# Two fused transformer layers on one core: layer-1 queries and position scores in an early pool, keys on Pool, experts three steps later

## The chip, the cores and the metric

The kernel runs on one core of a Trainium2 chip. The time is device microseconds (us) of that core for one execution of the whole program, with all inputs in the chip's own memory at the start and the output written back to it at the end. Engines are named as the profile names them: PE (TensorE, with PEld for its weight loads), DVE (VectorE), ACT (ScalarE), POOL (GpSimd) and SP (SyncE, which here only issues transfers, in the order of its own queue).

## What is computed

The input is two batches of 1024 tokens with 128 features, float32 throughout. Two layers follow each other, and each adds attention and a mixture of experts, both taken from the same normalized input, to that input.

```python
xn = _layernorm(x, axis=-1)
x = x + _L0_attn_ref(xn, ...) + _L0_ffn_ref(xn, ...)
xn = _layernorm(x, axis=-1)
x = x + _L1_attn_ref(xn, ...) + _L1_ffn_ref(xn, ...)
```

Layer 0's attention has 16 heads of 8 features, sigmoid scores and a causal mask; its experts are 32, computed densely and weighted, and one shared expert. Layer 1's attention is a softmax over all 1024 keys with a position term that depends on the clipped distance of query and key:

```python
att_rel_pos = jnp.einsum('bhsd,pd->bhsp', q, pos_emb_k)
att_idxs = jnp.clip(ar[None, :] - ar[:, None], -r, r - 1) % P     # r = 128, P = 256
att_pos = att_rel_pos[:, :, ar[:, None], att_idxs]
att = jax.nn.softmax((attn_val + att_pos) * attn_scale, axis=-1)
```

Layer 1's experts are 16 with 4 chosen for each token, and a shared expert of 352 hidden features that every token passes through.

## The kernel before, in words

**Order of the work.** Every PE instruction is placed by hand (`manual_schedule` for PE). The other engines are scheduled by a planner from the dependences, so their queues can stand in another order than the text; each engine then executes its own queue strictly in order. The program has two PE loops.

**The first loop** counts steps c. Each of the first 192 (`N_ATT`) makes one tile of layer 0's attention (`scores0`, `values0`) and opens or closes units of a feed-forward block. A unit (`open_unit`, L333) is a pair of products of 512 tokens with up to 128 hidden features (L341, L342), a sigmoid on ACT and two products on DVE; `close_unit` (L358) multiplies the result with the second weight and accumulates (L367). Units without biases (L346 to L349) are those of layer 1's shared expert, twelve in all: three parts for each of four blocks of 512 tokens. A dictionary `extra` (filled by `at(c, f, ...)`) says which other functions run at which step, and `due` says how many units may be open by then.

After step 192 comes the transition: `added0` and `merged0` of batch 1 add layer 0's two outputs and normalize again (L235 writes the normalized `xn1`), the pool `l0` is closed and `l1` opened on the same memory (`opened1`, which also clears sixteen `negmax` tiles on POOL, L776), and layer 1's attention is prepared. That preparation is what a dictionary `begin` lists for negative steps; the last loop lines before `manual_schedule` spread it over the steps up to `LAST`.

**Layer 1's attention** runs in the second loop, 128 steps (16 groups of one batch, one of four head sets and one half of the queries; 8 key tiles each). Four heads are computed at once, in four row groups of PE. A step t does:

- `scores` of its key tile: transposes of `near` (L936) and products of queries and keys (L946), then exponentials on ACT (L953);
- `values` of the step before (L965);
- `scan` of a tile ten steps ahead (`LEAD` = 10): products of queries and keys (L885), whose row maxima DVE takes, with `near` added where query and key are close (L905), or straight from PSUM (L910). `augment` (L920, L924) puts the maxima into the queries as an extra feature.

**Where `near` comes from.** `positions(n, pair)` multiplies queries with position vectors (L845), copies the result to `rel` on ACT (L849), fills its tail on DVE (L851), writes it to a scratch tensor in memory (`bounce`, L858) and reads it back skewed (`near`, L864). The last two are transfers on SP's queue, and the second waits for the landing of the first. Step 8n - 13 + 4 pair has the positions of group n, except that those of (1, 1) are at step 0.

**Operands.** `projections(b)` makes queries, keys and values of a batch; `operands(b, s)` makes one head set's masked queries `qs` (L820), two keys `kls` and `khs` (L824) on DVE and values `vs` on POOL (L827). In the second loop it stands 17 steps ahead of its group.

**Layer 1's experts.** Routing (`gate1`, `sort1`) is a sequence of small DVE operations, let go piece by piece. Then POOL scatters every token to its four slots (L618, two each step from `SCATTER` on), and at step `EXPERTS` the attention pauses: PE computes 79 blocks of 128 slots, each with weights that POOL fetches with an indirect transfer (L660). Tokens are loaded four blocks at a time on SP's queue (`fetch_x`, L670) and results stored there (L714). From then on POOL gathers the results, 64 in all (L630), scales and adds them (L640, L641). `paced` ties each scatter and gather to the last exponential of its step. When a quarter of the tokens (half of batch 0) is complete, `result` (L646) stores it, again on SP's queue.

Of the kernel before, what the change touches and what calls it, by code (L numbers as in the profile page):

```python
# [10 lines left out]
F32 = mybir.dt.float32  # L11
# [6 lines left out]
P = 128  # L18
D = 128
# [27 lines left out]
def fused_layers_kernel(ctx: ExitStack, tc: tile.TileContext, a: dict, out: bass.AP):  # L47
# [41 lines left out]


    banks = psum_pools(3, 1, 1, 0)
    l0_pool = tc.tile_pool(name="l0", bufs=1)
    l0 = l0_pool.__enter__()

# [238 lines left out]
    def open_unit():  # L333

        (m, wa, wb, w2m, ba, bb, rows), xT, tok = units[len(opened)][:3]
        if rows is not None:
            cb = moe.tile([P, TB], F32, tag="cb", name="cb", bufs=3)
            for lo, hi, src in rows:
                nc.sync.dma_start(cb[lo:hi, :], src[tok:tok + TB].partition_broadcast(hi - lo))
        hh = big()  # L340
        nc.tensor.matmul(hh[0:m, 0, :], wa, xT, start=True, stop=True)  # L341
        nc.tensor.matmul(hh[0:m, 1, :], wb, xT, start=True, stop=True)  # L342
        sg = moe.tile([P, TB], F32, tag="sg", name="sg")
        t = moe.tile([P, TB], F32, tag="t", name="t")
        h = moe.tile([P, TB], F32, tag="h", name="h", bufs=4)
        if ba is None:  # L346
            nc.scalar.activation(sg[0:m], hh[0:m, 0, :], AF.Sigmoid)
            nc.vector.tensor_mul(t[0:m], hh[0:m, 0, :], sg[0:m])
            nc.vector.tensor_mul(h[0:m], hh[0:m, 1, :], t[0:m])  # L349
        else:  # L350
            nc.scalar.activation(sg[0:m], hh[0:m, 0, :], AF.Sigmoid, bias=ba)  # L351
            nc.vector.scalar_tensor_tensor(t[0:m], hh[0:m, 0, :], ba, sg[0:m], ALU.add, ALU.mult)  # L352
            nc.vector.scalar_tensor_tensor(h[0:m], hh[0:m, 1, :], bb, t[0:m], ALU.add, ALU.mult)  # L353
        if rows is not None:
            nc.gpsimd.tensor_mul(h[0:m], h[0:m], cb[0:m])  # L355
        opened.append(h)
# [436 lines left out]
        return slice(32 * r, 32 * r + 32)  # L793

    def projections(b):
        l1 = pools["l1"]
        qf = l1.tile([P, T], F32, tag="qf", name="qf")
        kf = l1.tile([P, T], F32, tag="kf", name="kf")
        v = l1.tile([P, NT, D], F32, tag="vf", name="vf")
        for q in range(NB):  # L800
            c = slice(q * TB, (q + 1) * TB)
            ps = small()
            nc.tensor.matmul(ps, wq, xT1[b][:, c], start=True, stop=True)
            nc.scalar.mul(qf[:, c], ps, 1.0 / math.sqrt(HD))
            ps = small()
            nc.tensor.matmul(ps, wk, xT1[b][:, c], start=True, stop=True)
            nc.vector.tensor_copy(kf[:, c], ps)
            ps = quads(small())
            for i in range(4):
                t = q * TB + i * P  # L810
                nc.tensor.matmul(ps[:, i, :], xT1[b][:, t:t + P], wv, start=True, stop=True)
            nc.scalar.copy(v[:, 4 * q:4 * q + 4, :], ps)
        full[b] = qf, kf, v

    def operands(b, s):

        l1 = pools["l1"]
        qf, kf, v = full[b]
        qs = l1.tile([P, T], F32, tag="qs", name="qs", bufs=2)
        nc.vector.tensor_scalar(qs, qf, mask[:, s:s + 1], None, ALU.mult)  # L820
        ks = []
        for i, name in enumerate(("kls", "khs")):
            t = l1.tile([P, T], F32, tag=name, name=name, bufs=2)
            nc.vector.tensor_scalar(t, kf, not_aux[:, s:s + 1], k_add[:, i, s:s + 1], ALU.mult, ALU.add)  # L824
            ks.append(t)
        vs = l1.tile([P, NT, D], F32, tag="vs", name="vs", bufs=2)
        nc.gpsimd.tensor_copy(vs, v)  # L827
        ones = vs.rearrange("p t (r c) -> p t r c", r=NG)[:, :, :, aux[s]:aux[s] + 1]
        nc.gpsimd.memset(ones, 1.0)
        head[b, s] = qs, ks[0], ks[1], vs  # L830

    n_rel = [0]

    def positions(n, pair):


        b, s, q = groups[n]
        l1 = pools["l1"]
        qs = head[b, s][0]
        ps = [t.rearrange("p (j w) -> p j w", j=2) for t in four_banks()]  # L840
        for j in range(2):
            t = q * TB + (2 * pair + j) * P
            for r in range(NG):
                g = rows_of(r)
                nc.tensor.matmul(ps[r][:, j, :], qs[g, t:t + P], posd[g, :], start=True, stop=True)  # L845
        rel = l1.tile([P, 2 * NG * NEAR], F32, tag="rel", name="rel")
        rel = rel.rearrange("p (j r w) -> p j r w", j=2, r=NG)
        for r in range(NG):
            nc.scalar.copy(rel[:, :, r, 0:2 * RAD], ps[r])  # L849
        for j in range(2):  # L850
            nc.vector.tensor_copy(  # L851
                rel[:, j, :, 2 * RAD:NEAR],
                rel[:, j, :, 2 * RAD - 1:2 * RAD].to_broadcast([P, NG, NEAR - 2 * RAD]),
            )
        for j in range(2):
            bounce = bounces[n_rel[0] % N_BOUNCE]
            n_rel[0] += 1
            nc.sync.dma_start(  # L858
                bounce[:, :, P - 1:P - 1 + NEAR].rearrange("r p w -> p r w"), rel[:, j, :, :]
            )  # L860
            slot = (4 * n + 2 * pair + j) % 10
            t = pools["l1" if slot < 6 else "late"].tile([P, NG, NEAR], F32, tag=f"near{slot}", name="near")
            skew = bass.AP(bounce.tensor, bounce.offset + P - 1, [[W - 1, P], [P * W, NG], [1, NEAR]])
            nc.sync.dma_start(t, skew)  # L864
            near[n, 2 * pair + j] = t

    def spans(lo, hi, cut):

# [140 lines left out]
    for n, (b, s, q) in enumerate(groups):  # L1009
        t0 = 8 * n - LEAD  # L1010
        if q == 0:
            if s == 0:
                at_step(t0 - 8, projections, b)
            at_step(t0 - 7, operands, b, s)
        for pair in range(2):

            at_step(0 if (n, pair) == (1, 1) else 8 * n - 13 + 4 * pair, positions, n, pair)
    for n, (b, s, q) in enumerate(groups):
        for m in range(8):
            if 8 * n - LEAD + m < 0:  # L1020
                at_step(8 * n - LEAD + m, scan, n, m // 2, m % 2)
    at_step(-2, augment, 0)


    gates = {}
# [46 lines left out]
        at(60 + 4 * i, regroup, i)  # L1072

    at(N_ATT, blocks1, 0)
    at(N_ATT + 2, added0, 1)
    at(N_ATT + 4, merged0, 1)
    at(N_ATT + 5, lambda: l0_pool.__exit__(None, None, None))
    at(N_ATT + 5, opened1)
    at(N_ATT + 9, turned1, 1)
    at(N_ATT + 9, blocks1, 1)  # L1080
    LAST = N_ATT + 22
    for t in sorted(begin):
        if t < 0:
            for f, args in begin[t]:
                at(LAST + t * (LAST - N_ATT - 6) // -min(begin), f, *args)

    with tc.manual_schedule(engines={mybir.EngineType.PE}):
        c = 0
        while c < LAST or closed[0] < len(units):
            for f, args in extra.get(c, ()):  # L1090
                f(*args)
            if c < N_ATT:
                scores0(c)
                due = max(0, c - U0 + 1)
                if due > HALF:
                    due = HALF + (due - HALF) * HALF // (N_ATT - U0 - HALF)
            else:
                due = len(units)
            fresh = len(opened) < due
            if fresh:  # L1100
                open_unit()
            if 0 < c <= N_ATT:
                values0(c - 1)
            if closed[0] < len(opened) - 2 or (not fresh and c >= N_ATT and closed[0] < len(opened)):
                close_unit()
            for entry in list(later):
                entry[0] -= 1
                if entry[0] < 0:
                    later.remove(entry)
                    entry[1](*entry[2])  # L1110
            c += 1
        for _, f, args in later:
            f(*args)
# [16 lines left out]

    SORT, SCATTER, EXPERTS = 1, 26, 8 * len(groups) // B
    aside = {}

    def beside(t, f, *args):
# [11 lines left out]
                return  # L1148

    for t in range(SORT, SCATTER - 1):  # L1150
        for i in range(1 + t % 2):
            beside(t, route_on)
    beside(SCATTER - 1, route_on, True)
    for i in range(NTT * K1):
# [4 lines left out]
        beside(EXPERTS - 1, fetch_w, i)  # L1159

    with tc.manual_schedule(engines={mybir.EngineType.PE}):
        for t in range(N_STEPS + 1):
            if t == EXPERTS:
                values(t // 8 - 1, NT - 1, whole)
                experts()
            before = begin.get(t, ())
            for f, args in before:
# [4 lines left out]


            n, kt = (t - 1) // 8, (t - 1) % 8
            halved = 0 < kt and t + 1 < N_STEPS and not is_near(t + 1) and not before
            if t and t != EXPERTS:
                values(n, kt, left if halved else whole)
            m = t + LEAD
# [79 lines left out]
```

## Time and profile before

Five runs: median 1355.3 us, from 1347.06 to 1363.21.

| what | value |
|---|---|
| time of the profiled execution | 1355.62 us |
| its span, first to last instruction | 1353.8 us |
| mean granted PE clock | 0.960 |
| PE busy | 1221.7 us (90%) |
| DVE busy | 781.9 us (58%) |
| ACT busy | 617.1 us (46%) |
| POOL busy | 417.5 us (31%) |
| last layer-0 attention matmul starts | 436.1 us |
| step 0 of layer 1's attention starts | 523.4 us |
| first expert matmul (transposes, L685) | 883.6 us |
| step 64, right after the experts | 1031.0 us |

Times in the table's last four rows are from the start of the span. Busy time counts compute instructions only; matmuls are pipelined and their ends are modelled, so a busy PE is not PE at its peak. In the timelines, a bracket at the end of a line gives how long the engine stood idle before it and what released it; `x8` means eight instructions merged into one line. SPq lines are issues on SP's queue, and their length is not that of the transfer. The granted clock is a share of full speed.

### The profile page before, as it was taken

The numbers are of one execution on the slowest core, as the hardware profiler recorded it, in microseconds if no ns is written. First come the engines' busy times: TensorE is split into PE (matmuls) and PEld (weight loads), VectorE is DVE, ScalarE is ACT, GpSimd is POOL, SyncE is SP. The second block draws the span as 40 slices with busy tenths as digits, with TensorE's granted clock in tenths as the row PEclk, the third lists the DMA queues.
The fourth block names the chain that finished last, engine by engine and source line by source line (L and its number), as shares of the span: only waits on it lengthen the run. The fifth ranks groups of instructions, "written<-read, shape, count | busy, mean of one in ns | idle before, by whom it ended". The sixth has DMA issues, their size and how long they took to land.

```text
span 1353.8 us, 22925 instructions
## 1 busy us (share of the span) xinstructions
PE 1221.7 (90%) x8567; PEld 578.9 (43%) x8567; DVE 781.9 (58%) x2211; ACT 617.1 (46%) x1086; POOL 417.5 (31%) x514
## 2 busy tenths in 40 slices
PE   5889999989999888898999999968899999979997
PEld 2323332333333435344444344468886444434443
DVE  7773333563333775868765656734455866656553
ACT  3634444535454322453554545433344554536453
POOL 1124243233332100000033433135553445545540
PEclk9889999999999996898998999989999999989998
DMA  6773121111110064453455554578883555455430
GB/s 176 187 208 83 57 59 52 39 32 47 41 49 21 1 206 124 138 177 113 143 167 172 187 191 139 185 234 253 256 260 99 176 164 178 135 185 167 153 104 17
DMA packets 142499, 181.76 MB, mean 134 GB/s; under 512 B 16436, under 2 KB 126260, under 8 KB 142132
## 3 DMA queue, kind: packets, MB, share of 16 engines
q1 hardware_dynamic: 131972, 147.30, 35.8%
q0 software_dynamic: 10416, 32.99, 7.8%
q8 instruction: 68, 1.11, 0.3%
q14 instruction: 43, 0.35, 0.1%
HBM read 110.81 MB, written 73.77 MB: 136 GB/s over the span
## 4 chain that ended last, share of the span: by engine, by line
PE 37%; DMA 8%; DVE 8%; issue 5%; ACT 3%; POOL 2%; SPq 0%; POOLq 0%; DVEq 0%; ACTq 0%
PE sm L946 10%; PE sm L885 8%; PE acc L965 8%; PE sm L936 6%; DVE maxima L910 3%; DMA bounce<-rel 3%; DMA near<-bounce 3%; PE sm L845 2%; DVE junk L905 2%; POOL blockw L660 2%; PE sm L695 1%; ACT p L953 1%; DMA blockw<-wx,weight_row 1%; POOL room L660 1%; ACT rel L849 1%
## 5 line engine op out<-in xcount | busy, mean ns | idle before, releaser
L953 ACT ACTIVATE p<-sm 128x512 f32<-128x512 f32 x512 | 265.0, 607 | 254.1 <-PE sm L946 245.5
L910 DVE TENSOR_REDUCE maxima<-sm 128x1 f32<-128x512 f32 (+3 forms) x472 | 226.6, 502 | 100.5 <-PE sm L885 97.4
L455 ACT ACTIVATE at<-big 128x1024 f32<-128x1024 f32 (+1 forms) x192 | 144.8, 808 | 150.8 <-PE big L449 145.0
L905 DVE CUSTOM_DVE_ANT_0 junk<-sm,near 128x384 f32<-128x384 f32 (+2 forms) x292 | 130.4, 446 | 64.8 <-PE sm L885 42.4
L965 PE MATMUL acc<-p,vs 128*32 128x512 f32 (+1 forms) x1288 | 146.8, 525 | 0.4 <-ACT yu L977 0.4
L355 POOL TENSOR_TENSOR h<-h,cb 128x512 f32<-128x512 f32 x64 | 83.3, 1301 | 196.6 <-DVE h L353 186.4
L936 PE MATMUL sm<-ident,near 128*128 128x128 f32 x704 | 110.1, 291 | 32.4 <-DVE maxima L905 17.8
L352 DVE SCALAR_TENSOR_TENSOR t<-big,b,sg 128x512 f32<-128x512 f32 x64 | 47.9, 749 | 158.2 <-ACT sg L351 158.2
L946 PE MATMUL sm<-qa,kls 32*128 32x512 f32 (+3 forms) x832 | 121.2, 565 | 0.0
L660 POOL DMA_INDIRECT blockw<-wx,weight_row x53 | 50.4, 952 | 215.9 <-DVE rel L851 165.1
L936 PEld LDWEIGHTS sm<-ident,near 128*128 128x128 f32 x704 | 79.6, 146 | 81.6 <-issue 36.5
L885 PE MATMUL sm<-kls,qs 32*128 32x512 f32 (+2 forms) x776 | 111.0, 576 | 2.6 <-DVE at L560 1.5
L618 POOL DMA_INDIRECT slots_x<-xn,slot_of x64 | 62.9, 983 | 143.2 <-ACT p L953 133.1
L449 PE MATMUL big<-qm,xT 32*128 32x512 f32 (+3 forms) x768 | 103.5, 554 | 3.2 <-ACT at L455 1.9
L475 PE MATMUL acc<-at,xn 128*32 128x512 f32 (+3 forms) x768 | 84.9, 515 | 5.6 <-POOL at L460 4.5
L341 PE MATMUL big<-xT,w 128*128 128x512 f32 x128 | 73.9, 660 | 16.0 <-DVE h L353 13.6
L849 ACT COPY rel<-sm 128x512 f32<-128x512 f32 x116 | 59.6, 600 | 62.4 <-PE sm L845 56.7
L640 POOL TENSOR_SCALAR got<-got,share 128x128 f32<-128x128 f32 x64 | 41.5, 649 | 123.0 <-DMA got<-slots_y,slot_of 122.6
L630 POOL DMA_INDIRECT got<-slots_y,slot_of x64 | 64.7, 1011 | 30.9 <-ACT p L953 19.7
L367 PE MATMUL ffn<-h,w 128*128 128x512 f32 x128 | 72.9, 652 | 0.0
L460 POOL TENSOR_SCALAR_AFFINE_SELECT at<-at 128x512 f32<-128x512 f32 x64 | 40.8, 638 | 101.2 <-ACT at L455 100.9
L885 PEld LDWEIGHTS sm<-kls,qs 32*128 32x128 f32 x776 | 38.3, 186 | 78.3 <-ACT p L953 16.4
(285 smaller groups left out, 1709.1 us busy)
## 6 DMA issues: line engine op xcount, KB each, us to landing
bounce<-rel SPq DMA_DIRECT2D x64, 768.0 KB
near<-bounce SPq DMA_DIRECT2D x64, 768.0 KB
cb<-cw SPq DMA_DIRECT2D x128, 128.0 KB
slots_x<-zeros SPq DMA_DIRECT2D x19, 256.0 KB
room<-slots_x SPq DMA_DIRECT2D x19, 256.0 KB
slots_y<-by SPq DMA_DIRECT2D x19, 256.0 KB
bounce<-zeros SPq DMA_DIRECT2D x40, 63.5 KB
w<-in_w_dram SPq DMA_DIRECT2D x2, 1024.0 KB
```

The costliest lines, as they stand in the source:

```text
L355: nc.gpsimd.tensor_mul(h[0:m], h[0:m], cb[0:m])
L449: nc.tensor.matmul(halves[r // 2][:, r % 2, off:TB], xT0[b][g, kt * P:(kt + 1) * P], masked[b, s][g, q * TB + off:(q + 1) * TB], start=Tru ...
L455: nc.scalar.activation(at[:, 2 * j:2 * j + 2, off:TB], sc[:, :, off:TB], AF.Sigmoid, scale=4.0 / math.sqrt(HD))
L475: nc.tensor.matmul(y[32 * r:32 * r + 32, off:TB], xn0[b][:, kt * P + 32 * r:kt * P + 32 * r + 32], at[:, r, off:TB], start=(kt == 0), stop ...
L660: nc.gpsimd.indirect_dma_start(t[:, 0:WX], None, wx[:, :], bass.IndirectOffsetOnAxis(ap=weight_row[:, i:i + 1], axis=0))
L885: nc.tensor.matmul(ps[r][:, (k0 - lo) * P:(k1 - lo) * P], qs[g, qt * P:(qt + 1) * P], (kh if far else kl)[g, k0 * P:k1 * P], start=True, s ...
L905: nc.vector.tensor_tensor_reduce(junk[:, 0:(k1 - k0) * P], part, near[n, i][:, r, w0:w0 + (k1 - k0) * P], 1.0, -BIG, ALU.add, ALU.max, mx[ ...
L910: nc.vector.tensor_reduce(mx[:, r, slot:slot + 1], part, AX.X, ALU.max)
L936: nc.tensor.matmul(ps[r][:, i * P:(i + 1) * P], near[n, i][:, r, w0:w0 + P], ident, is_transpose=True, start=(i == close[0]), stop=False, ...
L946: nc.tensor.matmul(ps[r][:, i0 * P:i1 * P], k[g, kt * P:(kt + 1) * P], qa[n][g, i0 * P:i1 * P], start=(m == 0 and not close), stop=(m == l ...
L953: e = nc.scalar.activation(p[:, r, :], ps[r], AF.Exp)
L965: nc.tensor.matmul(y[rows_of(r), part], vs[:, kt, rows_of(r)], probs[n, kt][:, r, part], start=(kt == 0), stop=(kt == NT - 1 and part.stop ...
```

## The change

It has these parts:

- A pool `early`, opened ahead of layer 0's, holds `qf`, `kf`, the projected values, `qs` and `rel`, which were in `l1`. So `projections(0)`, `queries(0, 0)` and the first three `by_position` stand ahead of `opened1` now.
- `operands` is split into `queries` and `operands`, and `positions` into `by_position` (up to the write of the bounce) and `near_by` (reading it back). Positions of (1, 1) are made in the transition; only their `near_by` is left ahead of step 0.
- The preparation has steps of its own instead of being spread; scans, one each step, alternate with units (`due`).
- A unit without biases copies its second factor on ACT and makes its last product on POOL, instead of two products on DVE.
- The keys of all head sets are made on POOL instead of DVE, and `kf` is copied on ACT.
- Routing is let go more slowly, `SCATTER` is 33 instead of 26 and `EXPERTS` 67 instead of 64; gathers and results, counted from `EXPERTS`, move with it.

```diff
+    early = ctx.enter_context(tc.tile_pool(name="early", bufs=1))
...
             nc.scalar.activation(sg[0:m], hh[0:m, 0, :], AF.Sigmoid)
-            nc.vector.tensor_mul(t[0:m], hh[0:m, 0, :], sg[0:m])
-            nc.vector.tensor_mul(h[0:m], hh[0:m, 1, :], t[0:m])
+            nc.scalar.copy(t[0:m], hh[0:m, 1, :])
+            nc.vector.tensor_mul(sg[0:m], hh[0:m, 0, :], sg[0:m])
+            nc.gpsimd.tensor_mul(h[0:m], t[0:m], sg[0:m])
...
-        qf = l1.tile([P, T], F32, tag="qf", name="qf")
-        kf = l1.tile([P, T], F32, tag="kf", name="kf")
-        v = l1.tile([P, NT, D], F32, tag="vf", name="vf")
+        qf = early.tile([P, T], F32, tag="qf", name="qf")
+        kf = early.tile([P, T], F32, tag="kf", name="kf")
+        v = early.tile([P, NT, D], F32, tag="vf", name="vf")
...
-            nc.vector.tensor_copy(kf[:, c], ps)
+            nc.scalar.copy(kf[:, c], ps)
...
+    def queries(b, s):
+
+        qs = early.tile([P, T], F32, tag="qs", name="qs", bufs=2)
+        nc.vector.tensor_scalar(qs, full[b][0], mask[:, s:s + 1], None, ALU.mult)
+        head[b, s] = (qs,)
+
     def operands(b, s):
...
-        qs = l1.tile([P, T], F32, tag="qs", name="qs", bufs=2)
-        nc.vector.tensor_scalar(qs, qf, mask[:, s:s + 1], None, ALU.mult)
...
-            nc.vector.tensor_scalar(t, kf, not_aux[:, s:s + 1], k_add[:, i, s:s + 1], ALU.mult, ALU.add)
+            nc.gpsimd.tensor_scalar(t, kf, not_aux[:, s:s + 1], k_add[:, i, s:s + 1], ALU.mult, ALU.add)
...
-    def positions(n, pair):
+    def by_position(n, pair):
...
-            bounce = bounces[n_rel[0] % N_BOUNCE]
+            bounce = bounce_of[n, pair, j] = bounces[n_rel[0] % N_BOUNCE]
             n_rel[0] += 1
             nc.sync.dma_start(
                 bounce[:, :, P - 1:P - 1 + NEAR].rearrange("r p w -> p r w"), rel[:, j, :, :]
             )
+
+    def near_by(n, pair):
+
+        for j in range(2):
+            bounce = bounce_of.pop((n, pair, j))
             slot = (4 * n + 2 * pair + j) % 10
...
+    def positions(n, pair):
+        by_position(n, pair)
+        near_by(n, pair)
...
+            at_step(t0 - 7, queries, b, s)
             at_step(t0 - 7, operands, b, s)
         for pair in range(2):
-
-            at_step(0 if (n, pair) == (1, 1) else 8 * n - 13 + 4 * pair, positions, n, pair)
...
+            at_step(8 * n - 13 + 4 * pair, positions, n, pair)
...
     at(N_ATT, blocks1, 0)
+    at(N_ATT, projections, 0)
+    at(N_ATT, queries, 0, 0)
+    at(N_ATT + 1, by_position, 0, 0)
     at(N_ATT + 2, added0, 1)
+    at(N_ATT + 2, by_position, 0, 1)
     at(N_ATT + 4, merged0, 1)
     at(N_ATT + 5, lambda: l0_pool.__exit__(None, None, None))
     at(N_ATT + 5, opened1)
-    at(N_ATT + 9, turned1, 1)
+    for pair in range(2):
+        at(N_ATT + 5, near_by, 0, pair)
+    at(N_ATT + 5, operands, 0, 0)
+    at(N_ATT + 5, by_position, 1, 0)
+    at(N_ATT + 6, near_by, 1, 0)
+    at(N_ATT + 8, turned1, 1)
     at(N_ATT + 9, blocks1, 1)
-    LAST = N_ATT + 22
...
+    for m in range(LEAD):
+        at(N_ATT + 7 + m, scan, m // 8, m % 8 // 2, m % 2)
+    at(N_ATT + 9, by_position, 1, 1)
+    at(N_ATT + 12, queries, 0, 1)
+    at(N_ATT + 12, operands, 0, 1)
+    LAST = N_ATT + 7 + LEAD
+    at(LAST - 2, augment, 0)
...
-                due = len(units)
+                due = 2 * HALF + (min(max(c - N_ATT - 1, 0), 2) if c < N_ATT + 7 else c - N_ATT - 4)
+            due = min(due, len(units))
...
-    SORT, SCATTER, EXPERTS = 1, 26, 8 * len(groups) // B
+    SORT, SCATTER, EXPERTS = 1, 33, 8 * len(groups) // B + 3
...
-        for i in range(1 + t % 2):
+        for i in range(1 + (t % 4 == 0)):
             beside(t, route_on)
...
+        near_by(1, 1)
         for t in range(N_STEPS + 1):
             if t == EXPERTS:
-                values(t // 8 - 1, NT - 1, whole)
+                values((t - 1) // 8, (t - 1) % 8, whole)
                 experts()
...
-            halved = 0 < kt and t + 1 < N_STEPS and not is_near(t + 1) and not before
+            halved = 0 < kt and t != EXPERTS and t + 1 < N_STEPS and not is_near(t + 1) and not before
```

## The prediction

> **What bounds the kernel now.** I read the page first, then busy time by stretch, then the timelines of PE, DVE, SP and POOL around the two places that the change moves.
>
> ```profile
> span 1353.8 us, 22925 instructions
> PE 1221.7 (90%) x8567; PEld 578.9 (43%) x8567; DVE 781.9 (58%) x2211; ACT 617.1 (46%) x1086; POOL 417.5 (31%) x514
> ```
>
> PE is the bound over the whole, so what counts is where PE stands idle or cold. Stretches (us; PE, PEld, DVE, ACT, POOL busy; granted clock; DMA share; GB/s):
>
> ```profile
> 457.90:483.10 25.20, 22.82 (x90) 11.30 (x90) 14.56 (x22) 10.27 (x17) 5.09 (x20) 0.93 0.33 96
> 483.10:523.40 40.30, 31.76 (x150) 14.53 (x151) 33.65 (x112) 5.34 (x11) 0.00 (x0) 0.76 0.56 175
> 523.40:885.00 361.60, 334.77 (x2705) 159.57 (x2705) 248.38 (x796) 177.79 (x341) 72.97 (x77) 0.95 0.49 158
> ```
>
> The last layer-0 attention matmul runs at 436.1, step 0 of layer 1 begins at 523.4: a transition of 87.3 us. In 483.1 to 523.4 DVE is busy 33.65 of 40.3 and PE waits for it at a clock of 0.76.
>
> The timelines of DVE, SP and PE say what starts that stretch and what ends it:
>
> ```profile
> 455.65 2.14 DVE L235 TENSOR_SCALAR xn<-x,ln_mv,ln_rstd 128x128 f32<-128x128 f32 x8
> ...
> 483.09 0.42 DVE L905 CUSTOM_DVE_ANT_0 junk<-big,near 128x256 f32<-128x256 f32 x1 [3.45 <-DMA near<-bounce]
> ```
> ```profile
> 473.33 0.94 SPq L858 DMA_DIRECT2D bounce<-rel  x2
> 477.76 3.74 SPq L864 DMA_DIRECT2D near<-bounce  x2
> ```
> ```profile
> 523.42 1.94 PE L936 MATMUL sm<-ident,near 128*128 128x128 f32 x8 [2.54 <-issue]
> ```
>
> The second norm (L235) ends at 457.8; only then is the l0 pool closed, l1 opened and the projections evacuated. Rel is ready at 473.3, and the first scan's `near` lands at 483.1. Ten scans follow on DVE.
>
> At the experts, SP (in order) and PE show:
>
> ```profile
> 889.62 4.85 SPq L864 DMA_DIRECT2D near<-bounce  x2
> 894.58 0.51 SPq L670 DMA_DIRECT2D room<-slots_x  x1
> ...
> 902.79 1.11 PE L685 MATMUL sm<-ident,room 128*128 128x128 f32 x4 [9.83 <-DMA room<-slots_x]
> ```
>
> `positions` of step 63 puts two bounce and two near transfers between the second and the third `fetch_x`; PE stands 9.83 us.
>
> In batch 1 the same queue is held again, by `result` waiting for POOL (timelines of POOL, SP and PE):
>
> ```profile
> 1180.51 0.45 POOL L641 TENSOR_TENSOR x<-x,got 128x128 f32<-128x128 f32 x1
> ```
> ```profile
> 1180.99 0.38 SPq L646 DMA_DIRECT2D out_dram<-x  x1
> 1181.42 1.11 SPq L858 DMA_DIRECT2D bounce<-rel  x2
> 1186.62 3.45 SPq L864 DMA_DIRECT2D near<-bounce  x2
> ```
> ```profile
> 1192.62 1.33 PE L936 MATMUL sm<-ident,near 128*128 128x128 f32 x4 [8.32 <-DVE maxima L905]
> ```
>
> The 32nd gather is added at 1181.0; only then does SP issue the store, and behind it the bounce of step 91, whose rel DVE (L851) had finished at 1172.1. PE pays 8.32 us. POOL's gathers are thus on the path, through SP.
>
> **The transition, part by part.** PE's instructions are the same in number, in another order. Durations are rows of the transition: a 512-column fp32 product 0.86 us, an ACT copy or activation of 128x512 0.59 (L347), a DVE product 0.69 (L348), rel on ACT 2.05, its fill on DVE 0.76.
>
> *Ahead of the norm.* In place of the first shared unit PE takes six projection groups, 434.3 to 439.8. The last attention values move from 436.1 to 439.8. The first positions (1.25) come before the two products that end layer 0's experts (443.3 and 444.3). On DVE both query products (0.75 each) and the first fill stand ahead of yT, which ends at 446.0 (442.1 now); POOL's addition (1.27) ends at 447.4. ACT has the first unit's sigmoid ahead of the second rel, so the second unit waits for its bank until 449.2; the transposes run to 452.0, the merged x is done at 453.6, the statistics, root and scale (2.1, then 0.4, 1.1 and 2.2 as now) end at 459.4. The norm is 1.6 us later than now.
>
> *After it.* Both rels have bounced by then. Near is issued at 459.5 and lands 5.3 us later (477.76 to 483.09 now): 464.8. Meanwhile POOL clears negmax (2.40, L776) and makes the keys.
>
> *Price of a key on POOL.* No row shows it. These are nearest:
>
> ```profile
> L640 POOL TENSOR_SCALAR got<-got,share 128x128 f32<-128x128 f32 x64 | 41.5, 649 | 123.0 <-DMA got<-slots_y,slot_of 122.6
> L641 POOL TENSOR_TENSOR x<-x,got 128x128 f32<-128x128 f32 x64 | 30.2, 472 | 5.3
> L827 POOL COPY vs<-vf 128x1024 f32<-128x1024 f32 x8 | 8.8, 1100 | 6.0 <-ACT vf L812 3.6 <-PE acc L965 2.4
> ```
>
> L640 is the same operation on an eighth of the columns, median 0.60. Low end: the other 896 columns at the copy's rate (1.05 us for 1024), 0.60 + 0.92 = 1.5 us. High end: in proportion, 8 x 0.60 = 4.8. I take the slope of POOL's products (0.46 us for 128 columns at L641, 1.27 for 512 at L486: 2.1 ns each): 0.60 + 896 x 0.0021 = 2.5 us.
>
> The Trainium skill (GPSIMD Engine Reference, section 4.1, Engine selection) speaks against both moves: ordinary elementwise work belongs on VectorE, two-input operations being about twice as slow on GpSimd, one-input ones about line rate. The first half agrees with the rows (1.30 us at L355, 0.69 at L349). By the second a key would be about 0.9 us (an estimate, 1024 columns at its 1.2 GHz), and the sum below some 6 us lower; the 0.60 us of L640 for 128 columns contradicts it, and the row decides.
>
> So keys end at 459.5 + 2.4 + 2 x 2.5 = 466.9, and the first scan begins there, not at 483.1. PE idles from 455.2 until then. After it PE has ten scans (1.05 each), ten units (1.82), ten closings (0.9), four transposes back (0.53), eight forward (1.0), one positions (1.25) and one augment (0.6): 10.5 + 18.2 + 9 + 2.1 + 1.0 + 1.25 + 0.6 = 42.7 us. DVE has scans of 2.5 to 3.2 (28), ten products (6.9) and copies (4): 39. They alternate over three two-bank tiles, so I add 5 us of gaps and 1.5 for the cold start: step 0 at 516.1 to 517. I take 517.0: **-6.4 us**. Bounds: 4.8 us keys begin the scans 4.6 later (-1.8); 1.5 us keys 2 earlier (-8.4); no gaps -13; the whole run of 42.7 at the 0.76 that the stretch shows now, 56 us, +0.5.
>
> *Moved at no price.* The second factor of a unit goes to ACT (0.59) and POOL (1.30 each), where a round of unit and scan takes over 4 us; POOL's products stand behind four keys and two copies until about 474.5, the first closing is needed at 481. If that cover went (keys of 4.8: 483), the closing would wait some 2 us.
>
> **Steps 0 on.** `positions(1,1)` leaves step 0: 16 matmuls, 2.3 us between scan and step 1 (530.2 to 532.8): **-2.3** (0 to -3). Keys of later heads leave DVE (12 x 0.81) and two copies; DVE is busy 248 of 361 us there and PE waited for it in only a few places (3.95 at 626.4, beside a sort and two keys): **-2** (0 to -4). The sort moves with its pace but stays on DVE; nothing taken.
>
> **Experts at step 67.** No positions falls on step 66; five `fetch_x` follow each other. The 9.83 us wait goes: **-10** (-6 to -11). The last scatter is paced by step 64, two steps of some 4.6 us ahead, and a scatter lands within a few us; nothing taken.
>
> **The queue behind the experts.** Gathers also start three steps later, but in the built program `result` still stands on SP ahead of the bounces of steps 79 and 91, as now. From the end of the experts (1031.0) to the step-91 bounce (1181.4) POOL's chain takes 150.4 us: 32 gathers, mostly each waiting for its own landing. That chain keeps its length and gains two keys, 5.0. But three steps fewer are left to hide it: step 67 begins at 1044.1, 13.0 us after 1031.0. The bounce comes 155.4 us after step 67 begins, now 137.3: **+18.0**, paid as two waits. First: step 79's store at 86.1 after step 67, near landing about 10.8 later at 96.9, needed at 1130.6 - 1044.1 = 86.5: 10 us. Then at step 94 the present 8.3 becomes 16. Behind it stand every later bounce and near on SP, then DVE's scans, then PE. Bounds 16 (keys 1.5) to 22.6 (4.8); a quicker gather chain would lower it, at the extreme to 0. Keys of head 3 come 175 us after step 67, before their scan. At the end POOL is done near 300 of 328: no new wait.
>
> **Sum**: -6.4 - 2.3 - 2 - 10 + 18.0 = -2.7 us. The profiled execution took 1355.6 (span 1353.8 plus 1.8), the median of five is 1355.3 (1347.1 to 1363.2). Forecast 1355.3 - 2.7 = 1352.6 us.
>
> **Rivals.** (1) *No hold behind the experts.* Gathers land sooner, or their lag is made up, and the store waits as little as now: -20.7, 1334.6; with half the hold 1343.6. For it: landings of 1.6 us where no near is in flight against 6.6 with one. Against it: 30.0 us of SP time already waiting for L641. (2) *POOL is too slow for keys*, the slower case: each us of a key costs 2 at the first scan and 2 at the held store. It decides from 2.5 + 2.7 / 4 = 3.2 us per key; at 4.8 the sum is -2.7 + 4.6 + 4.6 = +6.5, 1361.8, and with the cold clock (+6.9 instead of its 1.5 allowance, at most) 1368.7. For it: L640's 0.60 us on 128 columns. Against: the copy's 1.05 for 1024. (3) *The early pool buys nothing*: the norm gates l1 as before and the scans stay DVE's: +3.7, 1359.0. Against: near lands 18 us earlier by the walk.
>
> **Chances.** About 1% (13.6 us) is what a measurement of this kernel can tell from no change. The sum's case, with (3) and the mild part of (2), 0.48 within 1%, its own range 1343 to 1362. Rival 1 beyond half, or transition gaps near none with quick keys: 0.30 faster. Rival 2 in full with the cold clock, or a wait that I missed on POOL's longer queue: 0.22 slower. Range 1336 to 1371, from most of rival 1 to rival 2.
>
> **What would show it.** Right: first scan's L905 near 467, step 0's L936 near 517, no wait above 2 us at L685, L646 about 86 and 155 us after step 67 with near waits of 10 and 16 us behind. A key on POOL outside 1.5 to 4.8 us moves the sum by 4 us for each. Wrong if L646 issues without waiting for L641, if PE idles at the first blocks for scatters, or if the scans still begin after 475.

## Result and profile after: slower by a quarter of a per cent

The changed kernel takes 1360.6 us (median of 52 runs, 1351.9 to 1368.7), the kernel before 1357.6 (94 runs). The ratio is 1.0025, its 95% interval 1.0013 to 1.0038, so the change costs 1.8 to 5.2 us. The forecast was a gain of 2.7.

The page's head, for the execution profiled:

```profile
span 1358.1 us, 22943 instructions
PE 1214.3 (89%) x8567; PEld 574.1 (42%) x8567; DVE 759.5 (56%) x2179; ACT 624.8 (46%) x1102; POOL 449.8 (33%) x542
```

DVE has lost 22 us of work and POOL gained 32, as intended; the span is 4.3 us longer all the same.

**The transition.** Busy time by stretch from the first scan to step 0 (us; PE, PEld, DVE, ACT, POOL; granted clock; DMA share; GB/s):

```profile
465.40:473.00 7.60, 7.27 (x28) 3.48 (x28) 3.58 (x13) 1.39 (x2) 5.69 (x7) 0.56 1.03 364
473.00:481.40 8.40, 5.95 (x32) 2.30 (x32) 5.87 (x16) 2.51 (x5) 2.52 (x2) 1.00 0.86 267
481.40:487.00 5.60, 5.53 (x22) 2.42 (x22) 1.65 (x7) 2.79 (x6) 0.00 (x0) 0.70 0.45 164
487.00:519.60 32.60, 31.82 (x133) 13.04 (x132) 27.43 (x83) 9.30 (x18) 8.86 (x7) 1.00 0.11 36
519.60:524.10 4.50, 1.84 (x7) 0.71 (x6) 1.37 (x2) 0.58 (x1) 1.26 (x1) 0.90 0.00 0
```

Before, DVE was the fuller engine of the stretch ahead of step 0 (33.65 of 40.3 us, PE 31.76). Now it is PE: it is busy 31.8 of the 32.6 us from 487.0 to 519.6. Two slices ahead of that run at a low clock (0.56 and 0.70). The timeline of PE shows the way in, a round in the middle, a scan behind transposes, and the tail:

```profile
465.44 1.33 PE L897 MATMUL big<-kls,qs 32*128 32x256 f32 x8 [8.19 <-POOL kls L829]
...
486.96 1.14 PE L897 MATMUL big<-khs,qs 32*128 32x512 f32 x8
488.19 1.10 PE L342 MATMUL big<-xT,sgw 128*96 128x512 f32 x2
489.12 1.02 PE L343 MATMUL big<-xT,suw 128*96 128x512 f32 x2
489.98 1.02 PE L369 MATMUL ffn<-h,sdw 128*128 128x512 f32 x2
490.93 1.14 PE L897 MATMUL big<-kls,qs 32*128 32x512 f32 x8
...
494.83 0.60 PE L744 MATMUL big<-ident,yT 128*128 128x128 f32 x4
495.36 1.92 PE L897 MATMUL big<-khs,qs 32*128 32x512 f32 x8
497.21 1.12 PE L342 MATMUL big<-xT,sgw 128*128 128x512 f32 x2
...
520.92 1.12 PE L369 MATMUL ffn<-h,sdw 96*128 96x512 f32 x2 [1.26 <-POOL h L351]
522.72 0.66 PE L744 MATMUL big<-ident,yT 128*128 128x128 f32 x4 [0.68 <-ACT yT L377]
524.16 0.69 PE L948 MATMUL sm<-ident,near 128*128 128x128 f32 x2 [0.78 <-DVE x L746]
```

PE stands idle for 8.19 us, with ten units still to do, until POOL has made a key. Then one round of scan, unit and closing takes 486.96 to 490.93, 3.97 us, with no gap. Step 0 starts at 524.16; before, it started at 523.42. The way in, on POOL and on ACT:

```profile
461.25 2.95 POOL L778 MEMSET negmax<- 128x128 f32 x16 [5.18 <-DVE xn L236]
464.20 1.18 POOL L829 TENSOR_SCALAR kls<-kf,not_aux,k_add 128x1024 f32<-128x1024 f32 x1
465.38 1.18 POOL L829 TENSOR_SCALAR khs<-kf,not_aux,k_add 128x1024 f32<-128x1024 f32 x1
```
```profile
450.59 2.05 ACT L852 COPY rel<-big 128x512 f32<-128x512 f32 x4 [3.27 <-DMA bounce<-rel]
```

A key takes 1.18 us. The norm ends at 461.1, 3.3 us later than before and 1.7 later than forecast. Ahead of it, `rel` has one buffer, so the second rel waits until the first bounce has been read out of it.

**The experts.** Five fetches follow each other (SP) and the 9.83 us wait is gone (PE):

```profile
889.70 13.42 SPq L672 DMA_DIRECT2D room<-slots_x  x5
```
```profile
892.77 0.63 PE L687 MATMUL sm<-ident,room 128*128 128x128 f32 x4 [0.93 <-DMA room<-slots_x]
```

**The held queue.** POOL, SP and PE around the first store of batch 0, and PE behind the second:

```profile
1111.64 1.20 POOL L829 TENSOR_SCALAR khs<-kf,not_aux,k_add 128x1024 f32<-128x1024 f32 x1
1112.83 1.19 POOL L829 TENSOR_SCALAR kls<-kf,not_aux,k_add 128x1024 f32<-128x1024 f32 x1
...
1117.56 0.45 POOL L643 TENSOR_TENSOR x<-x,got 128x128 f32<-128x128 f32 x1
```
```profile
1118.04 0.38 SPq L648 DMA_DIRECT2D out_dram<-x  x1
1118.47 1.43 SPq L861 DMA_DIRECT2D bounce<-rel  x2
1124.59 2.82 SPq L872 DMA_DIRECT2D near<-bounce  x2
...
1186.60 0.38 SPq L648 DMA_DIRECT2D out_dram<-x  x1
```
```profile
1130.26 2.04 PE L848 MATMUL sm<-posd,qs 32*128 32x256 f32 x10 [9.50 <-DVE maxima L917]
...
1197.82 1.34 PE L948 MATMUL sm<-ident,near 128*128 128x128 f32 x4 [9.65 <-DVE maxima L917]
```

The sixteenth addition ends at 1118.0, with two keys among the gathers; the store is issued at 1118.04 and the bounce at once behind it. PE waits 9.50 us for the scan that needs this `near`, and again 9.65 us behind the second store (1186.60).

### The profile page after: what moved, and what is told of

Same layout as the page of the kernel before. It is cut to its first block, busy times and chain, and to the rows that moved or that the text cites. A ratio compares the mean times of both kernels' runs of the same rounds, so it can differ in the third digit from the quotient of the medians.

```text
span 1358.1 us, 22943 instructions
## 1 busy us (share of the span) xinstructions
PE 1214.3 (89%) x8567; PEld 574.1 (42%) x8567; DVE 759.5 (56%) x2179; ACT 624.8 (46%) x1102; POOL 449.8 (33%) x542
## 4 chain that ended last, share of the span: by engine, by line
PE 60%; DVE 16%; DMA 11%; issue 5%; ACT 4%; POOL 4%; SPq 1%; POOLq 0%; DVEq 0%; ACTq 0%
PE sm L958 9%; PE sm L897 7%; PE acc L977 7%; PE big L342 6%; PE big L343 5%; PE big L451 4%; PE acc L477 4%; PE sm L948 4%; PE ffn L369 4%; DMA got<-slots_y,slot_of 3%; DVE maxima L922 3%; PE sm L697 2%; DMA bounce<-rel 2%; DMA blockw<-wx,weight_row 2%; DMA near<-bounce 2%
## 5 line engine op out<-in xcount | busy, mean ns | idle before, releaser
L848 PE MATMUL sm<-posd,qs 32*128 32x256 f32 x448 | 57.8, 418 | 17.5 <-DVE maxima L917 14.3
```

## The experiments

Each kernel is compared with the kernel before on the same chip, whose median there was 1358.5, 1353.0 or 1357.0 us; ratios are therefore what to compare. The stages of one profiled execution of each (us; for kernels with experts at step 64, the 13.0 us that steps 64 to 66 take in the kernel before are moved from the last column to the second):

| kernel | step 0 starts | steps 0 to 66 | experts | step 67 to end |
|---|---|---|---|---|
| before | 523.4 | 373.2 | 147.4 | 309.7 |
| changed | 524.2 | 368.6 | 141.5 | 323.8 |
| s1 store off SP | 522.4 | 372.3 | 134.5 | 304.9 |
| s2 before, store off SP | 525.7 | 371.4 | 147.9 | 298.2 |
| s3 before, experts later | 526.3 | 373.8 | 138.8 | 318.9 |
| s4 changed, experts at 64 | 521.7 | 371.0 | 145.3 | 310.5 |
| u1 changed, DVE as before | 521.2 | 376.2 | 134.3 | 325.7 |
| t1 units ahead | 515.0 | 370.8 | 136.7 | 325.8 |
| c1 = s1 + t1 | 519.1 | 372.8 | 136.4 | 302.2 |
| c2 = c1, later keys on DVE | 519.8 | 370.8 | 136.0 | 305.5 |
| c3 = c1, experts at 64 | 519.6 | 370.2 | 147.1 | 302.9 |
| c4 = c1, products on DVE | 517.7 | 368.1 | 138.6 | 304.2 |
| c5 = c1, positions later | 522.2 | 375.3 | 137.5 | 302.9 |

The same stage of the same code differs by some 4 us from one execution to another, and by 7 in the experts (141.5 in changed, 134.5 in s1), so single cells are read with that in mind. Nor is the profiled execution always near the median: that of s2 took 1345.0 us (median 1354.9), that of u1 1359.1 (median 1350.8).

**s1: the two stores of batch 0 on POOL's queue.**

```diff
-            result(0, t // 4)
+            result(0, t // 4, nc.gpsimd)
...
-    def result(b, q):
-        nc.sync.dma_start(out[b, ...
+    def result(b, q, queue=nc.sync):
+        queue.dma_start(out[b, ...
```

> The changed kernel, with the two stores of batch 0's finished halves issued on POOL's queue, right behind POOL's own last addition, and no longer on SP's. Nothing else differs. Theory (the held queue): the bounces of steps 79 and 91 no longer stand behind a store that waits for POOL, so PE's waits of 9.50 us near 1130 and 9.65 near 1198 both shrink to under 2; from step 67 to the end 309 us instead of 323.8; time 1360.6 - 15 = 1345.6, about 0.991 of the kernel before. Rival (the gathers themselves, or their pace by the exponentials, slow the rest): the waits stay or come back elsewhere, and the time stays within 3 us of 1360.6.

Measured: 1341.5 us, ratio 0.988 (0.9843 to 0.9916). PE's waits from step 67 on, in the changed kernel and then in s1 (us in total, times, longest):

```profile
PE sm L948 <- DVE maxima L917: 14.7, 8, 9.7
PE sm L848 <- DVE maxima L917: 9.5, 1, 9.5
```
```profile
PE sm L948 <- DVE maxima L917: 5.3, 9, 2.4
PE sm L897 <- POOL kls L829: 4.4, 1, 4.4
```

Both long waits are gone, and only these two stores were moved. That the order on SP's queue held the kernel is shown. The gathers themselves did not get faster: the stores come 86.9 and 161.0 us after step 67, in the changed kernel 83.7 and 152.3. A key behind them now costs 4.4 us, far less than the hold.

**s2: the same edit on the kernel before.**

> The kernel before, with the same two stores on POOL's queue. Theory (the held queue): its one wait of 8.32 us at step 94 goes, the first hold is covered there already: 1357.6 - 8 = 1349.6. Together with the run on the changed kernel: three steps later costs nothing once the queue is free, so that the changed kernel is then some 4 us the faster of the two. Rival: no change, 1357.6 within 3.

Measured: 1354.9 us, ratio 0.9976 (0.9948 to 1.0004): 0 to 7 us of gain, less than the 8 expected and not clear of nothing by the time alone. In its profile the 8.32 us wait is gone, none of `scores` for a scan is above 1.4 us from step 67 on, and the last stage is 11.5 us shorter. Against s1 it is some 13 us slower: with the queue free, the change is worth that much, three times the 4 us of the theory.

**s3: the kernel before with SCATTER 33, EXPERTS 67 and the slower routing only.**

> The kernel before, with only the third part of the change: SCATTER 33, EXPERTS 67, routing let go more slowly. Theory: experts 6 us shorter (no positions between the fetches), hold 13.0 us longer because the gather chain has three steps fewer: 1357.6 - 6 + 13 = 1364.6, 1.005 of the kernel before, with PE waits of 7 and 13 us or so behind the two stores. Rival (the hold comes from the keys or the products on POOL): the waits stay as before, time 1351.6.

Measured: 1359.0 us, ratio 1.0001 (0.9976 to 1.0027). Neither theory's number: the mechanism is there, its size is smaller.

```profile
PE sm L936 <- DVE maxima L905: 17.5, 7, 13.3
PE sm L845 <- DVE maxima L905: 6.2, 1, 6.2
```

The waits are 6.2 and 13.3 us as expected (7 and 13). Experts gain 8.6 and the last stage loses 9.2: gain and hold cancel. The keys and products stand on DVE here, so the rival falls: the hold comes without them.

**s4: the changed kernel with SCATTER 26, EXPERTS 64 and the old routing.**

> The changed kernel with the third part of the change undone: SCATTER 26, EXPERTS 64 and the old pace of the routing; the early pool, the engine moves and the new transition stay. Theory (the parts add up): the wait for the third fetch comes back (about 9 us), the hold of the stores falls from some 19 us of PE waits to the old 8 plus the two keys on POOL (2.4), so the time is 1360.6 + 9.8 - 12.6 = 1357.8; what is left against the kernel before is the transition (-2), steps 0 to 66 (-2) and the keys (+2.4). Rival (the new transition or the engine moves cost the time): 1361 or more.

Measured: 1351.7 us beside 1353.0, ratio 0.9992 (0.9967 to 1.0017). The theory's 1357.8 against 1357.6 is a ratio of 1.000, inside the interval; the rival's (1.0025 or more) is outside. The wait for the third fetch is back (9.9 us). So with the experts at step 64 the new transition and the engine moves are no loss, and next to no gain.

**t1: four units ahead of the first scan.**

```diff
+    def more_units():
+        for _ in range(4):
+            open_unit()
...
+    at(N_ATT + 7, more_units)
...
-    ... if c < N_ATT + 7 else c - N_ATT - 4)
+    ... if c < N_ATT + 7 else c - N_ATT)
```

> The changed kernel, with the four remaining shared units of batch 0 opened ahead of the first scan, where PE stands idle for 8.2 us, and not between the scans. Theory (after the first scan PE is the bound of the transition): four units of 2.1 us leave that stretch, step 0 near 516 instead of 524.2, time 1360.6 - 8 = 1352.6. Rival (DVE's maxima, POOL's products or the three PSUM tiles set the pace of the rounds): step 0 stays within 2 us of 524, time within 2 us of 1360.6, or later if the first scan has to wait for the units' products.

Measured: 1353.9 us beside 1358.5, ratio 0.9977 (0.9946 to 1.0008); step 0 at 514.96, and 517.7 to 519.8 in the four other kernels that contain the edit with the positions where they were. Mean 518.2, against 522.3 in the four kernels with the units between the scans (changed, s1, s4, u1): 4 us less. The stretch from the first scan to step 0 did lose the theory's 8 us: it takes 50.4 us on the mean, against 58.9. But the first scan starts 4.4 us later (467.9, against 463.5), because PE has the four units to do ahead of it and stands 2 to 3 us among them for a sigmoid that waits behind `rel` on ACT. So PE's list after the first scan did set the length of that stretch, and half of the gain was paid back at its start.

**u1: keys, products and the copy of kf on DVE again.**

> The changed kernel with the moves between engines undone: the keys and both products of a shared unit on DVE again, kf copied by DVE. Theory (PE is the bound after the first scan, DVE has 19 idle us of 59 there): step 0 stays within 3 us of 524; the two stores come 2.4 us earlier for want of the two keys on POOL; time 1360.6 - 2 = 1358.6. Rival (DVE becomes the bound of the transition again without the moves): step 0 near 530, time 1364 or more.

Measured: 1350.8 us beside 1353.0, ratio 0.9992 (0.9968 to 1.0015). From the first scan to step 0:

```profile
465.00:521.10 56.10, 50.84 (x208) 21.04 (x200) 46.62 (x131) 10.93 (x19) 3.49 (x8) 0.93 0.37 127
```

DVE has 46.6 us to do in place of 39.9, PE is still the fuller engine, and step 0 is not later. The rival falls: the moves to POOL and ACT buy no time here. They may even cost some: u1's ratio is 0.0033 (4.5 us) below the changed kernel's 1.0025, where the theory took 2 us, though the two intervals still overlap a little. Where that comes from is not shown. The waits behind the two stores are not shorter (6.9 and 13.4 us, for 9.50 and 9.65).

**c1: s1 and t1 together.**

> Both repairs on the changed kernel: the stores of batch 0 on POOL's queue and four units ahead of the first scan. Theory (two stages that have nothing to do with each other, so the gains add): 1341.5 - 6.7 = 1334.8, about 0.983 of the kernel before. Rival (units ahead only move the wait): 1341 again.

Measured: 1327.9 us beside 1353.0, ratio 0.9808 (0.9768 to 0.9847). The gains add: s1's and t1's ratios together give 0.983, inside the interval. This is the lowest ratio of all, well ahead of both kernels.

**c2: c1 with the keys of the second loop on DVE.**

```diff
+        eng = nc.vector if "late" in pools else nc.gpsimd
...
-            nc.gpsimd.tensor_scalar(t, kf, not_aux...
+            eng.tensor_scalar(t, kf, not_aux...
```

> As the run before in this call, with the keys of all head sets made in the second loop on DVE again; the first two head sets, made in the transition, stay on POOL. Theory: with the stores off SP's queue, PE waits 4.35 us for a key that stands behind POOL's gathers (near 1211 us); that wait goes, and the gather chain is 2.4 us shorter: 1334.8 - 4 = 1330.8. Rival: DVE's maxima come later by the keys (0.8 us each, 12 of them) and give it back: 1334.8 or more.

Measured: 1330.8 us, ratio 0.9834 (0.9804 to 0.9864), no faster than c1. The theory fell at its premise: the 4.4 us wait for a key, seen once in s1, did not come up in c1.

**c3: c1 with the experts back at step 64.**

> The changed kernel with both repairs (stores of batch 0 on POOL's queue, four units ahead of the first scan), but with SCATTER 26, EXPERTS 64 and the old pace of routing. Theory: with the queue free nothing holds the later experts' gain back, so going back costs the fetch wait of about 9.8 us against the repaired kernel at step 67 (0.981 of before): 0.988 of the kernel before. Rival (the later step is worth nothing even with a free queue): 0.981 again.

Measured: 1345.3 us beside 1357.0, ratio 0.9924 (0.9886 to 0.9961), 1.2% above c1's ratio. PE's wait for the tokens, in c3 and then in c1:

```profile
PE sm L687 <- DMA room<-slots_x: 9.3, 1, 9.3
```
```profile
PE sm L687 <- DMA room<-slots_x: 0.7, 1, 0.7
```

The experts themselves take 10.7 us longer in c3's profile than in c1's, and the stage behind them is no shorter. Three steps later is worth about 10 us or more, once nothing takes it back; by the two ratios it is some 16, with an uncertainty of about 7.

**c4: c1 with a unit's products on DVE.**

> The repaired kernel with both products of a shared unit on DVE again and no copy on ACT; keys stay on POOL. Theory (DVE has room in the transition, and the unit's chain loses 0.58 on ACT or POOL's slower 1.27 for DVE's 0.69): step 0 within 2 us of 519, time within 2 us of 0.981 of before. Rival (with units ahead of the scans DVE is near its bound, 38 busy of 47 to 51 us): the rounds wait for DVE, step 0 4 us or more later, 0.984.

Measured: 1334.9 us, ratio 0.9835 (0.9792 to 0.9878), step 0 at 517.7 (c1 519.1). Not to be told from c1; the rival's later step 0 did not come.

**c5: c1 with the last two position products behind the first scans.**

```diff
-    at(N_ATT + 5, by_position, 1, 0)
-    at(N_ATT + 6, near_by, 1, 0)
...
-    at(N_ATT + 9, by_position, 1, 1)
+    at(N_ATT + 9, by_position, 1, 0)
+    at(N_ATT + 10, near_by, 1, 0)
+    at(N_ATT + 11, by_position, 1, 1)
```

> The repaired kernel with the third and fourth position products moved behind the first scans (steps N_ATT + 9 and + 11 in place of + 5 and + 9). Theory: rel has one buffer, so the third rel waits on ACT for the second bounce to have been read, and the sigmoid of a unit behind it holds PE for 3.0 us near 461; that wait goes, the four units end some 2.5 us earlier and the first scan starts near 465 in place of 467.7; 1.25 us of products come into the stretch that PE bounds: net -1.5, 0.980. Rival (keys and near gate the scan anyway): only the 1.25 us are seen, 0.982.

Measured: 1341.0 us, ratio 0.9862 (0.9821 to 0.9904), no faster. The first half of the scan starts as early as hoped, and the second half waits (PE, then ACT):

```profile
463.65 0.70 PE L897 MATMUL big<-kls,qs 32*128 32x256 f32 x4 [0.68 <-POOL kls L829]
468.95 0.80 PE L897 MATMUL big<-kls,qs 32*128 32x256 f32 x2 [4.60 <-DVE sg L350]
```
```profile
467.03 0.60 ACT L348 ACTIVATE sg<-big 128x512 f32<-128x512 f32 x1 [5.89 <-POOL h L351]
```

The third of the four units cannot have its sigmoid until POOL's product of the first has freed a buffer of `sg`, and in POOL's queue that product stands behind the clearing of negmax, two keys and a copy (it starts at 465.74). The unit keeps its PSUM tile meanwhile, and the scan waits for one. The ACT wait that I took for the limit had covered this one.

## Why the prediction was wrong, step by step

Means over the profiles above, beside the prediction's terms:

| term | predicted | measured |
|---|---|---|
| transition (before, s2, s3 against changed, s1, s4) | -6.4 | -2.4 |
| steps 0 to 66 (same, with t1 and c1) | -4.3 | -1.7 |
| experts (four kernels at step 64, nine at 67) | -10 | -9.8 |
| hold, from step 67 to the end (before, s4 against changed, t1, u1) | +18.0 | +15.0 |
| sum | -2.7 | +1.1; by the time +3.4 (1.8 to 5.2) |

What the sum leaves open, 2 us, is within the scatter of single profiles.

**The step that failed** is "10.5 + 18.2 + 9 + 2.1 + 1.0 + 1.25 + 0.6 = 42.7 us ... so I add 5 us of gaps and 1.5 for the cold start". The stretch took 58.7 us in the changed kernel, and 59.4 in s1 and 59.6 in s4, not the 50.1 from 466.9 to 517.0. In the changed kernel PE was busy 52.4 of it. At the granted clocks of the stretches shown, the cold ones lost 7.27 x 0.44 + 5.53 x 0.30 = 4.9 us (an estimate), where I had 1.5. That leaves 47.5 us of PE work where my list had 42.7. The list was complete, but its rows were too short, the scans above all: a round is 3.97 us and not 3.77, scans over both keys go up to 1.45 instead of 1.05, and the two behind transposes take 1.85 (495.36 to 497.21 is one; why is not settled). The gaps are 6.3 for 5, the tail with POOL's product, ACT's copy and DVE's addition in a row among them. Even the bound that I gave, 56 us, was short of 58.7. The early start was real (the first scan at 465.4, forecast 466.9), but it came with the units held back behind it, and PE, idle for 8 us before, had too long a list after. I counted the moved instructions and saw both engines near 40 us, but did not ask which work PE could have done while it stood. t1 shows it: with four units ahead of the first scan the stretch is 8.5 us shorter, and step 0 comes at 518.2 on average.

**Smaller misses.** I took a key at 2.5 us, from L640's 0.60 us and the slope of the products at L641 and L486; it takes 1.19, below my low end of 1.5. The Trainium skill (GPSIMD Engine Reference, section 4.1) puts one-input work at about line rate, some 0.9 us by my estimate; the measured figure lies nearer to it than to my 2.5 us. The mistake was to scale a 128-column operation by the slope of a two-input one: 0.60 us for 128 columns and 1.18 for 1024 make most of the 0.60 a fixed cost (an estimate, if the two differ in size alone). The two keys ahead of the first scan saved 2.6 us by that, and most of it went again: the norm ended at 461.1, not 459.4, with the wait for the single `rel` buffer that I had not followed ahead of it.

Of the -2 for keys off DVE in the steps, no trace is seen: steps 0 to 66 take 368.1 to 375.3 us in kernels with all keys on POOL, and 370.8 and 376.2 in c2 and u1, where the later keys are on DVE. Whether `positions(1, 1)` gave its 2.3 is not settled on its own.

**What was right.** The experts' gain, to 0.2 us on the mean; the changed kernel's own profile alone would give 5.9. The hold: that POOL's gathers hold PE through SP's queue is shown by s1, and rival 1 (no hold) is out. Its size was less sure: three steps alone cost 9.2 us in s3, where I had 13.0, and with keys on DVE (u1) the last stage is as long as with them on POOL, so what makes up the rest of the 15.0 is open. The first store came 83.7 us after step 67 (86 predicted) and the second at 152.3 (155); the waits were 9.50 and 9.65, for 10 and 16. The second was too large by 6 us, part of it probably because PE came later there: it ran the 11.8 us behind the first wait at a clock of 0.68.

Among the rivals (3) came nearest in time (1359.0), but not in its reason: the first scan did come 13 us earlier (PE at 465.4, before at 478.4), and DVE was not the bound, as u1 shows. The sign turned because the transition gained 4.0 us less than forecast and the steps 2.6 less, which is more than the 3.0 by which the hold was over-priced.

## What to carry to other kernels

A store that waits for a slow engine belongs on that engine's queue, not ahead of transfers that others wait for: two such stores cost the changed kernel some 20 us (s1) and hid the worth of the later experts. When a gate is moved forward, list what each engine still has to do behind it, and check which of that could run while the engine now stands idle ahead of it. A gain that comes from moving a stage to a later step is paid back where a chain of fixed length behind it then has fewer steps to hide it: the experts' 10 us went that way.

## What the hardware showed

A short wait of PE can be followed by a loss longer than itself. t1 and c1 run the same PE instructions from the first scan to step 0 (57, 36 and 109 in three stretches), and the granted clock tells them apart (t1, then c1, columns as above):

```profile
467.50:479.50 12.00, 8.36 (x57) 4.17 (x56) 9.42 (x29) 3.07 (x6) 6.90 (x7) 1.00 0.94 301
479.50:488.40 8.90, 8.85 (x36) 3.91 (x36) 5.48 (x13) 3.77 (x8) 1.27 (x1) 1.00 0.67 234
488.40:514.90 26.50, 23.67 (x109) 9.92 (x108) 23.23 (x76) 6.28 (x12) 6.33 (x5) 1.00 0.01 2
```
```profile
467.70:481.00 13.30, 9.81 (x57) 5.20 (x57) 9.55 (x29) 3.31 (x6) 7.15 (x8) 0.87 0.94 304
481.00:492.60 11.60, 11.60 (x36) 5.23 (x36) 5.54 (x13) 3.78 (x8) 1.27 (x1) 0.71 0.45 153
492.60:519.10 26.50, 23.66 (x109) 9.92 (x108) 23.25 (x76) 6.26 (x12) 6.32 (x5) 1.00 0.00 0
```

The last 26.5 us are alike to 0.02 us; ahead of them c1 loses 1.3 and 2.7 us with its clock at 0.87 and 0.71. In slices of 0.2 us, c1's clock is 0.50 from 470.7 to 474.1 and from 481.0 to 487.8, that is for 3.4 and 6.8 us, and 1.00 in the rest of the three stretches; in t1 it is 1.00 throughout. The wait just ahead of the second spell is 1.53 us, and it is the longest since the first scan; t1 has the same wait without a spell, so what sets one off is not shown. The same code can come out 4 us apart in this place, which is one reason why single profiles of a stage differ.

The Trainium skill (TensorE: Matmul & The Clock Gate, Part 1: The HAM clock gate) says that the clock falls to half after an idle window of about 3.4 us, and that the window runs freely, so that the same kernel can differ from run to run. The second half agrees with this pair in that the two differ, and spells of 3.4 and 6.8 us are one and two windows of that length. By the first, taken as a window without PE work, c1's clock should not have fallen behind waits of at most 1.53 us, and there the measurement decides.
